# A third order for the opening of a fused linear-attention kernel: products made in terms beside the scans, and unit 0 worked under the first substitution

## The chip, the cores and the metric

The kernel runs on one core of a Trainium2 chip. The metric is the device time of one execution in microseconds (us). All data is 32-bit floating point (f32). The engines are called as the profile calls them: PE (TensorE, matrix products; PEld is its loading of weights), DVE (VectorE), ACT (ScalarE), POOL (GpSimd), and SP (SyncE), which in this kernel issues nearly all DMA transfers. Each engine works through its own queue in order; an instruction that waits holds up everything behind it on that engine.

## The reference, cut to what matters

The inputs are x and fside (4 batches of 512 tokens by 512 channels), cond (4 by 128) and weights. Two blocks follow each other, `x = x + attn(cond1(x))` and `x = x + ffn(cond2(x))`:

```python
# condition ("bi-wkv"): k = v = fside; scans over the tokens, forwards and backwards
decay = exp(-exp(w)) * (0.5 + 0.5 * tf);   ek = exp(min(k, 30));   ekv = ek * v
nf, df = scan(a = a * decay + ekv, b = b * decay + ek)     # and nb, db from the other end
euk = exp(min(u + k, 30))
out = sigmoid(x) * (nf + nb - ekv + euk * v) / max(df + db - ek + euk, 1e-8) * (0.8 + 0.2 * tf)

# attention: 16 query/key heads, 32 value heads of 128
qkvz = c @ W_qkvz.T;  beta, g = sigmoid(b), -exp(A_log) * softplus(a + dt_bias)  # from c @ W_ba.T
q, k, v = silu(causal_conv_of_4_taps(qkv));  q, k normalised
# chunks of tokens: M = strictly lower part of (k beta) k^T * decays, T = (1 + M)^-1,
# then a recurrence over the chunks with a state of 128 x 128 per value head
out = (norm(core) * norm_w * silu(z)) @ W_out.T
```

The ffn is a product with binarised weights. What the change touches is the first batch's condition, the gates (beta, g), and the first heads of the attention.

## The kernel before, in words

The work is cut into 64 *units*: four batches by 16 query/key heads, each unit with its key, query, two values and two z slices. A unit needs four *projections* of 128 weights by 512 tokens (r = 0 query, 1 key, 2 and 3 the values), each four products of 128x128 by 128x512 that add in a PSUM bank (`project`, halves 0 and 1 of two products each), and its z products (`z_product`). In the first batch the weight *slab* of 128 rows is loaded (`slab_start`, raw tile of a pool `ld` with four buffers), transposed on PE (`slab_turn`), copied by ACT (`slab_end`) and stored to a DRAM scratch `wsc` for the later batches; load and store are both issued by SP.

The convolution is `tap` 0 on ACT and taps 1 to 3 on DVE (`taps`); `silu`, `square` and the norm's sum (`norms`, `norms_copy`, `norms_turn`) follow. For a key, `key_norm` and `key_root` make an inverse square root (three Newton steps of four small POOL operations, `root`) and `key_factors` its products with the gates. `gap_load` brings the unit's cumulated decays by a broadcast DMA (512 KB), from a DRAM tile `gsc` that the gates write once per batch; `gap_mask` (POOL, 128x1024) and `gap_exp` (ACT, eight exponentials of 128x128 with a bias each) make decay matrices of them, "d" for keys (`dkd`) and "t" for queries (`dkt`). `key_pairs` (PE) and `key_matrix` (DVE, 8 steps) give M, and `key_blocks` writes its diagonal blocks of 32 to DRAM (four DMAs).

The inverse of M is made in two stages. For each *group* of four units, `group_load` brings all 128 diagonal blocks, one per partition, and `group_step` runs a substitution over 30 columns, two small operations each; `group_end` writes the result back. `inverse_load` (seven DMAs) brings the blocks of a unit, and `inverse_1` to `inverse_4`, each a set of small products on PE with a copy on DVE behind it, build the inverse of the whole chunk from them. Then the chunks follow (`chunk_r`, `chunk_w`, `chunk_t`): product with the state, product with the inverse (`ps_w`), new state and output. ACT and DVE make the steps between.

The order is written out by hand. `InOrder` keeps every engine's instructions in program order, apart from what the framework moves within its own constraints; `plan` lists in 21 lines (*slots*) what one *iteration* i does for several units at once: the chunks of unit i-1 (C), the values, query and inverse of unit i (F), the key of unit i+6 (K, `AHEAD`), the end of unit i-2 and the output product of unit i-3. `jobs` adds single items to a slot.

Before iteration 0 stands an *opening*, since nothing is there yet to overlap:

- the first batch's condition for its four columns of 128 channels (`first_turn` to `first_end`): transposes of fside and x on PE, exponentials on ACT, four scans of 128x512 per column on DVE, products on POOL, the sums of the scans as products with the identity on PE (`first_sum`: three terms each, `ps_d_first` and `ps_n_first`), a reciprocal on DVE, and the result in `cT`. The slabs of six keys are turned among it (`slab_turn(turned, 1)`);
- the gates of batch 0: `gates_product` over all four columns (`ps_ba`), `gates_exp`, `gates_series` (first beta, then a logarithm's series on DVE), `gates_sum`, `gates_keep`, `gates_turn`, `gates_rows` (the write to `gsc`);
- the keys of units 0 to 3 (*group 0*) and of 4 and 5 (*others*): `first_key`, `first_conv`, `first_silu`, `first_norm`, `first_root`; the matrices of group 0; its substitution on DVE; the norms and matrices of the others around it;
- then iteration 0, which makes the values, query and inverse of unit 0 and the key of unit 6, with the inverse moved behind slot 18 (`later`). The z products of unit 0 come in iteration 1.

In the profile L80 is the line of `InOrder`'s lambda, so that nearly every instruction has that line and is told by its tile: `lent_*` the condition's tiles, `wraw`/`wsc`/`w` a slab raw, stored and turned, `ps_p` projections, `ps_kk` key pairs, `L`, `t`, `Lt` the substitution, `ps_i` and `ps_j` the inverse's steps, `ps_w` both the turned slabs and the products with the inverse.

Of the kernel before, what the change touches and what calls it, by code (L numbers as in the profile page):

```python
# [9 lines left out]
F32 = mybir.dt.float32  # L10
# [30 lines left out]
def kernel(  # L41
# [104 lines left out]
    with ExitStack() as main:  # L146
# [24 lines left out]
        for cb in range(KT):  # L171
            at = slice(cb * P, (cb + 1) * P)
            raw = ld.tile([P, NC, P], F32, tag="raw", name=f"raw_k_first_{cb}")
            for t, src in ((raw, fside), (xs[0][:, :, at], x)):
                A.dma_start(out=t, in_=src[0, :, at].rearrange("(c p) d -> p c d", p=P))
            first_raw[cb] = raw

# [4 lines left out]
        for n, v in enumerate((w1, w2, u1, u2)):  # L182
            Q.dma_start(out=wu[:, n, :], in_=v.rearrange("(n p) -> p n", p=P))
        Q.dma_start(out=alog, in_=A_log.partition_broadcast(P))
# [17 lines left out]
        A.activation(nea, alog, AF.Exp)  # L202
        V.tensor_scalar_mul(nea, nea, -1.0)

# [127 lines left out]

        def gates_series(g):

            b, y, e = g["b"], g["y"], g["e"]
            V.tensor_scalar_add(beta[b], beta[b], 1.0)
            V.reciprocal(beta[b], beta[b])
# [21 lines left out]
        def gates_keep(g):  # L359
# [13 lines left out]
                gsum[b][:, 0].rearrange("p c (q r) -> p q c r", r=2),  # L373
            )

        def gates_turn(g):
            g["pt"] = bank("pj", f"ps_gt_{g['b']}")
            T.transpose(g["pt"][: NC * HV, :P], g["flat"][:, : NC * HV], ident)

        def gates_rows(g):  # L380
            b, n = g["b"], NC * HV
            rows = wkp.tile([P, S], F32, tag="d", name=f"sp_r_{b}")
            A.copy(rows[:n, :P], g["pt"][:n, :P])
# [137 lines left out]
        def root(v, y, t):  # L521
            for _ in range(3):
                G.tensor_tensor(t, y, y, ALU.mult)
                G.tensor_tensor(t, t, v, ALU.mult)
                G.tensor_scalar(t, t, -0.5, 1.5, ALU.mult, ALU.add)
                G.tensor_tensor(y, y, t, ALU.mult)
# [491 lines left out]
        def last_add(b, c):  # L1018
# [79 lines left out]
        INVERSE = (  # L1098
            inverse_1, inverse_1_end, inverse_2, inverse_2_end, inverse_3, inverse_3_end,
            inverse_4, inverse_4_end,  # L1100
        )

# [27 lines left out]
        for i in range(2):  # L1130
            homes.append(u2p.tile([P, S], F32, tag="q", name=f"lent_q_{i}"))

# [10 lines left out]
        def first_bound(w):  # L1143
# [3 lines left out]
            w["nf"] = w["ek"]  # L1147
# [14 lines left out]
        def first_scan(w, what):  # L1162
            dec = decay[:, 0, w["cb"], 0:1].to_broadcast([P, S])
            src = w["ek" if what == "d" else "ekv"]
            V.tensor_tensor_scan(w[what + "f"], dec, src, 0.0, ALU.mult, ALU.add)
            V.tensor_tensor_scan(
                backwards(w[what + "b"]), dec, backwards(src), 0.0, ALU.mult, ALU.add
            )

        def first_mix(w):  # L1170
            G.tensor_tensor(w["ekv"], w["ek"], w["k"], ALU.mult)
            G.tensor_tensor(w["d"], w["d"], w["ek"], ALU.subtract)
            G.tensor_tensor(w["k"], w["d"], w["k"], ALU.mult)

        def first_sum(w, what):
            ps = w["sum_" + what] = bank("st", f"ps_{what}_first_{w['cb']}")
            parts = (w["d" if what == "d" else "k"], w[what + "f"], w[what + "b"])
            for i, part in enumerate(parts):
                T.matmul(ps, lhsT=ident, rhs=part, start=(i == 0), stop=(i == 2))

        def first_end(w):
# [5 lines left out]

        work = []
        stages = (
            first_turn, first_bound, first_limit, first_x, first_mix, (first_scan, "d"), (first_sum, "d"),  # L1190
            (first_scan, "n"), (first_sum, "n"), first_end,
        )
        for cb in range(KT):
            w = wkv_start(0, 0, cb)
            for i, f in enumerate(stages):
                work.append((i + 4 * cb, cb, f, w))
        turned = 0
        for i, (_, cb, f, w) in enumerate(sorted(work, key=lambda s: s[:2])):
            f, *args = f if isinstance(f, tuple) else (f,)
            f(w, *args)  # L1200
            if i % 6 == 5 and turned < AHEAD:
                if turned == 0:
                    for n in range(AHEAD):
                        if n < 2:
                            slab_start(n, 1, homes[n])
                if turned + 2 < AHEAD:
                    slab_start(turned + 2, 1, homes[turned + 2])
                slab_turn(turned, 1)
                slab_end(turned, 1)
                turned += 1  # L1210
        for n in range(turned, AHEAD):
            slab_turn(n, 1)
            slab_end(n, 1)


        wba_raw = ld.tile([2 * HV, D], F32, tag="raw", name="wba_raw")
        Q.dma_start(out=wba_raw, in_=W_ba)
        wbaT = wp.tile([P, KT, 2 * HV], F32, name="wbaT")
        ps = bank("pj", "ps_wba")
        for k in range(KT):  # L1220
            T.transpose(
                ps[:, k * 2 * HV : (k + 1) * 2 * HV], wba_raw[:, k * P : (k + 1) * P],
                ident[: 2 * HV, : 2 * HV],
            )
        A.copy(wbaT.rearrange("p k o -> p (k o)"), ps[:, : KT * 2 * HV])

        cw = wp.tile([P, 4 * HQ, 4], F32, name="cw")
        Q.dma_start(out=cw, in_=conv_w.rearrange("(n p) k -> p n k", p=P))
        g = {"b": 0}

        def first_key(n, tag="pp"):
            project(n, 1, 0, tag)
            project(n, 1, 1, tag)

        def first_conv(n):
            tap(n, 1, 0)
            taps(n, 1)

# [213 lines left out]
```

## Time and profile before

| | us |
|---|---|
| median of 3 runs (lowest to highest) | 3196.23 (3192.85 to 3197.49) |
| the profiled execution: its time | 3197.57 |
| its span | 3195.8 |
| PE busy in the span | 3069.3 (96%), 20058 instructions |
| DVE busy | 2044.6 (64%) |
| ACT busy | 1861.6 (58%), of it 137 table loads 175.8 |
| POOL busy | 1329.4 (42%) |
| mean granted PE clock over the span | 0.981 |

The profile is one execution. Times in it count from the span's start. A product's idle time is put down to what released it; PE's matrix products of f32 show as two records each. A granted clock below 1.00 means that PE ran slower in that stretch. The page's 40 slices are 80 us each: PE's busy tenths are 6, 4, 8 in the first three and 9 in all others but the last, which has 8.

### The profile page before, as it was taken

To read this page: it belongs to the slowest core of one execution; us is meant where nothing else is said; L and a number is where in the kernel's file an instruction comes from. 1 tells how busy PE (TensorE), PEld (TensorE's weight loads), DVE (VectorE), ACT (ScalarE), POOL (GpSimd) and SP (SyncE) were. 2 spreads that over 40 slices of the span, in tenths; PEclk is the share of its full clock that TensorE was granted. 3 is DMA by queue.
4 is the path that set the end of the run, shared out by engine and by line. 5 is a ranking of instruction groups with operands and counts; after the bars stand their busy time and mean duration, and the time that the engine had idled before them with its cause. 6 is when DMAs were issued, how large, how long until landed. Compare 5 with 4: busy or idle time off the path is not lost.

```text
span 3195.8 us, 57474 instructions
## 1 busy us (share of the span) xinstructions
PE 3069.3 (96%) x20058; PEld 2055.2 (64%) x20058; DVE 2044.6 (64%) x4454; ACT 1861.6 (58%) x5115; POOL 1329.4 (42%) x3042
## 2 busy tenths in 40 slices
PE   6489999999999999999999999999999999999998
PEld 3356766666766666666666666666666666665664
DVE  7545767666655776667655686667755656577542
ACT  2446666666666666556565666556666555655542
POOL 3216354263522646264432646255442515255302
PEclk9689999999999999999999999999999999999999
DMA  3334444444434323332332323323332332333321
GB/s 74 95 87 130 141 127 119 124 125 128 132 109 142 115 59 106 86 96 78 108 102 78 116 86 83 111 77 95 112 92 76 104 86 86 105 90 93 105 83 53
DMA packets 418800, 320.49 MB, mean 100 GB/s; under 512 B 217104, under 2 KB 326160, under 8 KB 418128
## 3 DMA queue, kind: packets, MB, share of 16 engines
q1 hardware_dynamic: 414288, 314.72, 33.6%
q8 instruction: 160, 2.62, 0.3%
q10 hardware_dynamic: 4224, 2.10, 0.2%
q14 instruction: 128, 1.05, 0.1%
HBM read 246.19 MB, written 70.52 MB: 99 GB/s over the span
## 4 chain that ended last, share of the span: by engine, by line
PE 80%; DVE 11%; ACT 3%; DMA 3%; issue 1%; SPq 1%; ACTq 0%; POOL 0%; DVEq 0%; POOLq 0%
PE ps_p L80 24%; PE ps_out L80 12%; PE ps_z L80 12%; PE ps_w L80 4%; PE ps_s L80 4%; PE ps_i L80 3%; PE ps_o L80 3%; PE ps_j L80 3%; DVE y L80 3%; PE ps_st L80 2%; PE ps_kq L80 2%; PE ps_f L80 2%; DVE f L80 2%; PE ps_h L80 1%; PE ps_v L80 1%
## 5 line engine op out<-in xcount | busy, mean ns | idle before, releaser
L80 PE MATMUL ps_p<-cT,w 128*128 128x512 f32 x2000 | 956.4, 606 | 8.4 <-ACT w L80 8.4
L80 DVE SCALAR_TENSOR_TENSOR y<-ps_p,cw,y 128x511 f32<-128x511 f32 (+2 forms) x768 | 570.9, 743 | 419.3 <-ACT y L80 405.6
L80 PEld LDWEIGHTS ps_p<-cT,w 128*128 128x128 f32 x2000 | 346.9, 191 | 302.0 <-issue 270.8
L80 PE MATMUL ps_z<-w,cT 128*128 128x256 f32 x2048 | 476.5, 379 | 0.0
L80 PE MATMUL ps_out<-wo,hT 128*128 128x512 f32 x1024 | 466.8, 599 | 7.3 <-DMA wo<-wosc 7.3
L80 PEld LDWEIGHTS ps_z<-w,cT 128*128 128x128 f32 x2048 | 373.7, 190 | 42.5
L80 PEld LDWEIGHTS ps_out<-wo,hT 128*128 128x128 f32 x1024 | 186.0, 191 | 195.8 <-issue 189.0
L80 POOL TENSOR_TENSOR L<-L,t 128x30 f32<-128x30 f32 (+14 forms) x450 | 270.4, 601 | 35.3
L80 ACT ACT_TABLE_LOAD x137 | 175.8, 1283 | 154.0 <-DVE y L80 116.0
L80 ACT ACTIVATE qs<-ps_s,eg 128x128 f32<-128x128 f32 x384 | 120.5, 366 | 229.5 <-DVE r L80 121.9
L80 POOL TENSOR_TENSOR t<-L 128x30 f32<-128x30 f32 (+14 forms) x450 | 228.7, 508 | 34.5 <-DMA L<-blocks_m 3.3
L80 POOL TENSOR_TENSOR rs_t_o<-rs_y_o 128x8 f32<-128x8 f32 x192 | 38.5, 201 | 461.0 <-DVE rs_y_o L80 450.0
L80 ACT ACTIVATE y<-ps_p,cw 128x512 f32<-128x512 f32 x256 | 174.1, 680 | 90.2 <-PE ps_p L80 90.1
L80 POOL TENSOR_SCALAR_AFFINE_SELECT dkd<-dkd 128x1024 f32<-128x1024 f32 x64 | 70.5, 1101 | 350.4 <-DMA dkd<-gsc 223.0
L80 ACT ACTIVATE dkt<-dkt,gsum 128x128 f32<-128x128 f32 x512 | 162.9, 392 | 69.3 <-POOL dkt L80 68.9
L80 DVE TENSOR_TENSOR x<-x,ps_out 128x512 f32<-128x512 f32 x256 | 168.9, 679 | 32.8 <-PE ps_out L80 32.6
L80 POOL TENSOR_TENSOR rs_t_k<-rs_y_k 128x4 f32<-128x4 f32 x174 | 48.3, 277 | 328.4 <-DVE rs_y_k L80 319.3
L80 DVE SCALAR_TENSOR_TENSOR o<-o,rs_y_o,nz 128x128 f32<-128x128 f32 x512 | 183.0, 412 | 0.1
L80 DVE SCALAR_TENSOR_TENSOR r<-ps_s,nbe,vb 128x128 f32<-128x128 f32 x384 | 115.9, 343 | 96.8 <-PE ps_s L80 96.7
L80 ACT ACTIVATE junk<-o 128x128 f32<-128x128 f32 x512 | 158.0, 309 | 31.8 <-DVE o L80 23.6
L80 DVE TENSOR_TENSOR o<-ps_o,qs 128x256 f32<-128x256 f32 x192 | 80.8, 421 | 144.1 <-PE ps_o L80 136.1
L80 ACT ACTIVATE wd<-ps_w,eg 128x128 f32<-128x128 f32 x384 | 119.7, 364 | 87.8 <-PE ps_w L80 87.5
(270 smaller groups left out, 5771.3 us busy)
## 6 DMA issues: line engine op xcount, KB each, us to landing
w<-wsc SPq DMA_DIRECT2D x288, 256.0 KB, 5.3
dkd<-gsc SPq DMA_DIRECT2D x64, 512.0 KB, 4.7
dkt<-gsc SPq DMA_DIRECT2D x64, 512.0 KB, 4.5
wraw<-in_L_attn_W_qkvz_dram SPq DMA_DIRECT2D x96, 256.0 KB, 3.0
wo<-wosc SPq DMA_DIRECT2D x96, 256.0 KB, 3.8
wsc<-w SPq DMA_DIRECT2D x90, 256.0 KB, 2.1
blocks_m<-dkd SPq DMA_DIRECT2D x256, 32.0 KB, 1.7
L<-blocks_m SPq DMA_DIRECT2D x16, 512.0 KB, 5.5
```

Source lines behind the costliest of these rows:

```text
L80: return lambda *args, **kw: tc.keep_in_program_order(op(*args, **kw))
```

## The change

The change rewrites the opening and removes iteration 0; from iteration 2 on the program is as before.

- Loads: ACT issues those of the first column only; SP issues the other six after `cond`, `w1`, `w2` and `u1`.
- Condition: the two subtractions per column on POOL go; `first_sum` has four terms each, the first multiplied by a tile `minus` (minus identity) on PE. All columns' transposes and exponentials come earlier (`1.5 * cb`).
- Slabs: eleven are turned in the condition, one behind each of its steps from step 4 on: keys 0 to 3, `W_ba`, unit 0's values and query (r = 2, 3, 0), keys 4 to 6.
- Gates and keys 0 to 2 are made by terms (`first_gates`, `first_key`): columns 0 and 1 together, column 2, column 3, each when the column is done, between the sums on PE.
- Gates: beta is made later (`gates_beta`), the cumulated sums are copied straight from PSUM, the transpose shares a bank, `nea` is made later (ACT, POOL).
- Keys: unit 0's value and query projections stand between the keys of group 0; the first root runs on DVE (`root(*many, V)`); keys 4 to 6 are projected under the substitution and convolved behind it.
- Under the substitution: unit 0's values, query, z products and `kq`; the inverse of unit 0 follows it directly, with the steps of keys 4 and 5 between its stages.
- Iteration 1 gets, as `jobs`, the matrices and blocks of keys 4, 5 and 6 and the remaining steps of 5 and 6; `is_made` leaves out z of unit 0 there.

```diff
-        for cb in range(KT):
+        def first_load(cb, queue):
...
+        first_load(0, A)
...
-        for n, v in enumerate((w1, w2, u1, u2)):
+        for n, v in ((0, w1), (1, w2), (2, u1)):
             Q.dma_start(out=wu[:, n, :], in_=v.rearrange("(n p) -> p n", p=P))
+        for cb in range(1, KT):
+            first_load(cb, Q)
+        Q.dma_start(out=wu[:, 3, :], in_=u2.rearrange("(n p) -> p n", p=P))
...
-                gsum[b][:, 0].rearrange("p c (q r) -> p q c r", r=2),
+                ps[:, :n].rearrange("p (c q r) -> p q c r", q=HQ, r=2),
...
-        def root(v, y, t):
+        def root(v, y, t, E=G):
...
         def first_mix(w):
             G.tensor_tensor(w["ekv"], w["ek"], w["k"], ALU.mult)
-            G.tensor_tensor(w["d"], w["d"], w["ek"], ALU.subtract)
             G.tensor_tensor(w["k"], w["d"], w["k"], ALU.mult)
...
-            parts = (w["d" if what == "d" else "k"], w[what + "f"], w[what + "b"])
+            if what == "d":
+                parts = (w["ek"], w["d"], w["df"], w["db"])
+                w["nf"] = w["ek"]
+            else:
+                parts = (w["ekv"], w["k"], w["nf"], w["nb"])
             for i, part in enumerate(parts):
-                T.matmul(ps, lhsT=ident, rhs=part, start=(i == 0), stop=(i == 2))
+                T.matmul(ps, lhsT=ident if i else minus, rhs=part, start=(i == 0), stop=(i == 3))
...
+        def first_gates(ks):
...
+            for k in ks:
+                for c in range(NC):
+                    T.matmul(
+                        ba[:, c, :], lhsT=cT[0][:, k, c * P : (c + 1) * P], rhs=wbaT[:, k, :],
+                        start=(k == c == 0), stop=(k == KT - 1 and c == NC - 1),
+                    )
...
+        def first_key(n, ks):
...
+            for k in ks:
+                T.matmul(
+                    u["pp1"], lhsT=u["w1"][:, k, :], rhs=cT[0][:, k, :], start=(k == 0),
+                    stop=(k == KT - 1),
+                )
...
+        slabs = [(lambda n=n: slab_start(n, 1, homes[n]), lambda n=n: slab_turn(n, 1), lambda n=n: slab_end(n, 1)) for n in group0]
+        slabs.append((wba_start, wba_turn, wba_end))
+        slabs += [(lambda r=r: slab_start(0, r), lambda r=r: slab_turn(0, r), lambda r=r: slab_end(0, r)) for r in (2, 3, 0)]
+        slabs += [(lambda n=n: slab_start(n, 1, homes[n]), lambda n=n: slab_turn(n, 1), lambda n=n: slab_end(n, 1)) for n in others[:2]]
+        slabs.append((lambda: slab_start(AHEAD, 1), lambda: slab_turn(AHEAD, 1), lambda: slab_end(AHEAD, 1)))
...
+        for i, f, *args in (
+            (13.5, first_gates, (0, 1)), (13.6, first_key, 0, (0, 1)), (13.7, first_key, 1, (0, 1)),
+            (13.8, first_key, 2, (0, 1)), (17.5, first_gates, (2,)), (18.1, first_key, 0, (2,)),
+            (18.2, first_key, 1, (2,)), (18.3, first_key, 2, (2,)),
+        ):
+            work.append((i, KT, f, *args))
+        loading, turning = list(slabs), list(slabs)
+        for start, *_ in slabs[:2]:
+            start()
+            loading.pop(0)
+        for i, cb, f, *args in sorted(work, key=lambda s: s[:2]):
+            f(*args)
+            if cb < KT and i >= 4 and turning:
+                if loading:
+                    loading.pop(0)[0]()
+                _, turn_it, end_it = turning.pop(0)
+                turn_it()
+                end_it()
...
+        first_silu(0)
+        tap(2, 1, 0)
+        both(project, 0, 2)
+        first_norm(0)
+        key_pairs(0, "st")
...
+        many = root_start(kn, GROUP * NC, "first")
+        root(*many, V)
...
+        tap(0, 3, 0)
+        tap(0, 0, 0)
+        taps(0, 3)
+        taps(0, 0)
...
         for j in range(1, BS - 1):
             group_step(0, j, V)
         group_end(0, V.tensor_copy)
         inverse_load(0)
         inverse_load(1)
...
+        first_conv(4)
+        inverse_1(0)
+        inverse_1_end(0)
+        inverse_2(0)
+        first_conv(5)
+        inverse_2_end(0)
...
+        for n, slot in zip(others, (0, 6, 12)):
+            job(1, slot, key_matrix, n, 0)
+            job(1, slot + 1, key_matrix, n, 1)
+            job(1, slot + 1, key_blocks, n)
+        for half in range(2):
+            job(1, 2, gap_exp, 5, "d", half)
+            job(1, 8, gap_exp, 6, "d", half)
+        job(1, 0, tap, 6, 1, 0)
+        job(1, 1, taps, 6, 1)
+        job(1, 2, silu, 6, 1)
...
-        for i in range(NU - W - 1):
+        for i in range(1, NU - W - 1):
```

## The prediction, made before the change was run

> **What bounds the kernel now.** I read the 40 slices first: from the fourth on PE is at 9, and only the first three show gaps. So a change of the opening is worth what it does until the units run at PE's pace. Then the busy time by stage, cut where the chain of waits changes hands: last column of the condition done (62.83), decays written out (77.28), blocks of the first group arrived (122.82), substitution done (145.88), first product with an inverse of unit 0 (199.12), of unit 1 (242.18), of unit 2 (290.27). Columns: stretch, its length, busy us of PE, PEld, DVE, ACT, POOL, then granted clock, DMA share, GB/s.
>
> ```profile
> 13.00:62.83 49.83, 34.34 (x98) 15.64 (x98) 49.02 (x38) 14.07 (x26) 22.21 (x12) 0.97 0.30 69
> 62.83:77.28 14.45, 11.71 (x50) 7.22 (x51) 9.37 (x27) 2.21 (x7) 0.00 (x0) 0.95 0.00 1
> 77.28:122.82 45.54, 31.86 (x113) 20.39 (x112) 20.55 (x50) 25.67 (x56) 14.15 (x36) 0.69 0.37 123
> 122.82:145.88 23.06, 8.10 (x24) 5.18 (x24) 21.00 (x63) 9.28 (x32) 0.00 (x0) 0.57 0.01 4
> 145.88:199.12 53.24, 29.53 (x198) 18.58 (x198) 19.04 (x48) 12.10 (x25) 8.16 (x37) 0.66 0.33 91
> 199.12:242.18 43.06, 42.03 (x298) 30.28 (x298) 21.69 (x51) 27.51 (x78) 5.43 (x18) 0.93 0.35 98
> 242.18:290.27 48.09, 44.05 (x314) 31.43 (x313) 23.28 (x59) 30.34 (x83) 29.23 (x70) 0.93 0.50 151
> 290.27:338.92 48.65, 48.65 (x338) 33.72 (x337) 36.27 (x73) 34.28 (x88) 29.27 (x58) 1.00 0.48 144
> ```
>
> DVE carries the sums (49.02 of 49.83) and the substitution (21.00 of 23.06); between and after, nobody is full; from 290 on PE is. The chain (start, length, engine and tile) names the waits:
>
> ```profile
> 94.57 9.55 PE ps_p L80 x16
> ...
> 119.10 3.69 DMA L<-blocks_m
> ...
> 155.61 3.11 DMA wraw<-in_L_attn_W_qkvz_dram
> ...
> 187.71 1.08 PE ps_i L80 x32
> ```
>
> The products of keys 4 and 5 (94.57) stand before the matrices of units 0 to 3, and a slab load starts unit 0's projections only after the substitution. From the timeline:
>
> ```profile
> 18.37 5.49 PE L80 MATMUL ps_d_first<-lent_M,ident 128*128 128x512 f32 x6 [3.00 <-POOL lent_M L80]
> ...
> 24.51 2.74 PE L80 MATMUL ps_n_first<-lent_M,ident 128*128 128x512 f32 x6
> ...
> 54.51 1.40 PE L80 MATMUL ps_d_first<-lent_vb,ident 128*128 128x512 f32 x2 [3.53 <-DVE lent_vb L80]
> ...
> 62.89 3.12 PE L80 MATMUL ps_ba<-wbaT,cT 128*128 128x64 f32 x26 [0.35 <-DVE cT L80]
> ...
> 206.66 0.57 ACT L80 COPY w<-ps_w 128x512 f32<-128x512 f32 x1
> ```
>
> A 512-wide f32 product is two records: 0.86 us at full clock (six records 2.74), 1.7 at half (5.49). After 3.53 us without work the granted clock fell to 0.50; after 2.66 us (before 42.43) it did not.
>
> **The change part by part**, against the profiled execution (3197.57 us, span 3195.8; 1.3 above the median).
>
> *Sums (+9.3).* ACT now issues two loads, not eight; its first load of tables, at 10.51 before, comes at about 2, and the first exponentials at 8 to 9 (limited by the landing of u1, 2.3 plus 5.2 to 6.9) instead of 12.37. DVE begins near 9.2, not 13.0: -3.8. The six moved loads are issued by SP instead (0.4 to 0.5 each, waiting on earlier landings as ACT's did), so its first slab load goes at 10.8 instead of 10.14. The two POOL subtractions per column become `minus` products on PE; POOL still runs two products of 2.1 us beside each second pair of scans, so those stay at 2.2 us against 1.2 alone, and I credit nothing. Against it: PE's order puts four key slabs and W_ba ahead of the first sum, where one slab stood. On SP, wraw_3 stands behind the store of slab 0, and that behind ACT's copy, which now follows the exponentials of three columns (15 activations, 2.8 us per column: about 17.5). wraw_3 issues at 18, lands 2.9 later; W_ba issues behind slab 1's store at 18.8 and lands 3.1 later, 22. The first sum, four products, starts at 22.7 and ends at 26.2 (full clock) to 29.5 (half); I take 28, since PE was at half until 24.3 before. DVE, through with its scans at 17.5, waits; its first end step comes at 28 instead of 24.27: +3.7. The order of SP is thus what the early start is lost to. Next, the key terms (0,1) stand between cT(1) and the third column's sums: gates 1.9 (16 records at 0.12) + six products 5.2 + sum 3.4 = 10.5 us, where DVE is ready at 7.2 (41.25 to 48.5 before): +3.3, and up to +7 at half clock, since PE idles 3.5 us there; I take +4.3. Term 2 adds 2.6 ahead of the last sum: +0.6. Three slab transposes (0.43 each) between the first column's two sums put the second 0.7 behind the reciprocal. 3.7 + 4.3 + 0.6 + 0.7 = 9.3. Ends: -1 (slabs on time, full clock) and +13 (all cold).
>
> The page "TensorE: Matmul & The Clock Gate" of the Trainium skill (Part 4) says that transposes do not count as work for the clock. By it the dense slab transposes would leave PE at half and the first sum at 29.5, 1.5 us more; no row here parts the two.
>
> *Gates (-3.3).* Of the gates' 32 records the first 24 are made beside the sums, so behind the last column stand 8 at 0.12, not 26 (3.12): -2.2. `gates_beta` behind the series: -0.6 (68.01 less 67.4). `sp_f` from PSUM without waiting for the copy: -0.5. Keys 0 to 3 (2.6 + 3.4) lie beside the series' 7 us on PE. Ends -2 and -4.
>
> *Keys to blocks (-5.3).* From the decays' write: DVE's taps for 1, 2, 3 and for unit 0's value hide nothing late. PE: value product from +0.6, cold after the gap (eight records 6.2), norm 0.95 and pairs 0.93, product 3.4, norm, pairs, product 3.4, norms: the norms are ready at +20.4. Root on DVE: three ops and twelve at 0.2, 3.1; POOL factors 0.9; 32 matrix steps 8.9 (as at 107.10); blocks out and in 6.8 (115.99 to 122.82): +40.2 against 45.5. ACT's 32 exponentials end at +22.6, POOL's seven masks (1.09 each, loads 1.3 apart) at +16.5 (two slab loads, put between the decay loads on SP, are in that): both beside it. The two unit-0 products before the norms are what is late now; without them -12. With PE at half throughout: +4.
>
> *Substitution (0).* The same 60 steps, 23.1. Under it go unit 0's z (four products 6.9), transposes and keys 4 to 6 (10.3): about 25 us of PE, from +27 to +56 after the write, done before +63.
>
> *To the first inverse product (-34.3).* From Lt: blocks 2.9, seven loads at 0.49 (2.95), landing 2.2: 8.2. The inverse chain took 9.5 (187.71 to 197.2); taps of key 5 stand before its second copy on DVE: +1.2. 18.9 against 53.24. Ends -31 (waiting on the loads for unit 1 too) and -37.
>
> *Unit 0's chunks, iteration 1 (+12).* PE loses z (6.9) and two slabs (0.9), gains two pairs (1.8) and norms: 37 us if PE were full. It will not be. DVE: key 4's matrix is first in the queue and waits for POOL's root, which starts late and has two masks inside: to +4.6; then eight matrix steps 2.2, taps of key 6 2.3, small ops 0.8: the state copy comes at +10.3, not +3.0 (202.15). ACT: two groups of eight exponentials (2.45 each), activations of key 6 (2.0) and, of the iteration's six table loads (two before, at 201.12 and 215.02), three before slab 7's copy, which comes at +16.3, not +7.5 (206.66), and PE waits behind it, cold when it resumes; key 6's exponentials and two loads push key 7's square and the next slab, so that unit 1's second projection starts at +36.7, not +21.0. From there 22 us less z and slabs, latency-bound, 19: 56. I take 55. Ends 40 (ACT's own work, 39) and 58.
>
> A table load is 1.28 us in this trace, the next activation starting at once (104.85 and 106.14): four make 5.1. "ScalarE: Activation LUTs" of the Trainium skill (What ACT_TABLE_LOAD costs) counts 2.66 per switch with its drain; by that the sum would be 5.5 worse. The row decides.
>
> *Iteration 2 (+3).* Blocks of key 7, then seven inverse loads, then unit 2's decays on SP come about 3.5 later against PE. It waits there already (250.79, 3.39 idle). Ends 0 and +6. Later iterations have the same instructions.
>
> Sum: 9.3 - 3.3 - 5.3 + 0 - 34.3 + 12 + 3 = -18.6. 3197.6 - 18.6 = 3179.0; taken from the median, 3177.6. I say 3178.
>
> **Rivals.**
> 1. *The fill works:* slabs arrive in time, PE stays warm, iteration 1 runs near ACT's own 40 us. Sums +2, gates -3.3, keys -8, inverse -35, iteration 1 -1, iteration 2 +2: -43, 3154. For it: 29.5 of the 53 us before the first inverse product were PE's, and that work is now under the substitution. Against: the orders above.
> 2. *It gives the gain back:* sums at +13, keys -1, iteration 1 +15, iteration 2 +6, with -3.3 and -34.3: -4.6, 3192. For it: every queue has more in front of it in just these stages.
> 3. *Slower, by slabs one at a time:* eleven slabs must pass PE before the second column's sum. If SP's store-before-load order leaves one in flight, a trip is 0.43 + 2.9 + 1.1 + 0.6 + 0.33 = 5.4 us, 59 in all, and that sum comes at 70 instead of 41: +29, total +10, 3207. It decides from trips of 5.0 us on (25 us late). Against: the order lets two be in flight, and loads were 2.9 us.
> 4. *No effect,* for PE is at 96% of the span: 3196. Against it: PE had no work for 23.7 of the 53.24 us from 145.88.
>
> **How the numbers follow.** Forecast (-33 to -6.4) 0.69; rival 1 0.15; rivals 2 and 4 0.09; rival 3 0.07. A measurement of this kernel tells about 0.2%, 6.4 us, from none. Faster 0.84, same 0.09, slower 0.07. The range cuts a tenth below and a tenth above: 3160 to 3191.
>
> **What would show it.** The last column's end near 71; `ps_d_first` first at 22 to 23, behind `ps_wba`; gsc near 82; L near 122; first `ps_i` near 154 and inverse product near 164; a PE gap of several us before `ps_p` of key 7 with ACT as releaser; unit 1's inverse product near 219. I am wrong if slabs come earlier (sums then end at 62) or if iteration 1 keeps PE full.

## The result, and the profile after

The changed kernel takes 3182.40 us (median of 7 runs, 3176.15 to 3188.74) against 3196.23 (median of 7, 3192.85 to 3201.87): a ratio of 0.9956, 95% interval 0.9944 to 0.9969. It is faster by 0.44%, and the interval lies below 1. The forecast was 3178, range 3160 to 3191.

The profiled execution took 3176.15 us (span 3174.2). It is the fastest of the seven; what that means is settled by one of the runs below. First the busy time by stage of this execution, cut at the same events as before: last column of the condition done (75.13), decays written (86.57), blocks of the first group arrived (124.63), substitution done (147.75), first product with an inverse of unit 0 (167.83), of unit 1 (222.51), of unit 2 (272.12). Columns as before: stretch, length, busy us of PE, PEld, DVE, ACT, POOL, granted clock, DMA share, GB/s.

```profile
13.00:75.13 62.13, 50.81 (x158) 27.49 (x158) 39.75 (x32) 11.61 (x22) 9.44 (x7) 0.89 0.41 91
75.13:86.57 11.44, 8.37 (x29) 4.35 (x29) 7.82 (x24) 2.77 (x8) 0.30 (x1) 1.00 0.00 1
86.57:124.63 38.06, 30.63 (x116) 17.78 (x116) 25.67 (x68) 25.39 (x61) 11.90 (x24) 0.87 0.49 161
124.63:147.75 23.12, 14.62 (x64) 10.56 (x64) 21.04 (x63) 9.97 (x24) 0.00 (x0) 0.86 0.09 28
147.75:167.83 20.08, 9.76 (x138) 8.05 (x138) 8.91 (x17) 4.80 (x8) 3.29 (x13) 0.50 0.48 137
167.83:222.51 54.68, 42.33 (x283) 27.83 (x283) 27.78 (x78) 37.85 (x99) 12.82 (x55) 0.81 0.19 54
222.51:272.12 49.61, 44.91 (x314) 32.16 (x314) 24.81 (x62) 29.85 (x82) 29.22 (x70) 0.92 0.51 152
```

In the first stretch the roles have changed: DVE had 49.02 of 49.83 us and now has 39.75 of 62.13, and PE has 50.81, so the three columns that became longer now wait for PE. The substitution has 14.62 us of PE under it, not 8.10. The stretch from 145.88 to 199.12, 53.24 us long, has become one of 20.08. The next one has grown from 43.06 to 54.68, with ACT at 37.85. Against the prediction (us; stage lengths after less before):

| stage | predicted | measured |
|---|---|---|
| sums | +9.3 | +12.3 |
| gates | -3.3 | -3.0 |
| keys to blocks | -5.3 | -7.5 |
| substitution | 0 | +0.1 |
| to the first inverse product | -34.3 | -33.2 |
| iteration 1 | +12 | +11.6 |
| iteration 2 | +3 | +1.5 |
| sum | -18.6 | -18.2 |

The sums, column by column (`cT` written, from DVE's timeline): first column at 29.18 before, 33.44 after; then 12.07, 12.07 and 9.51 us for the next three before, and 12.08, 16.46 and 13.14 after. The first column waits for its sum on PE, which stands behind `W_ba`:

```profile
23.84 0.43 PE L80 MATMUL ps_wba<-ident,wba_raw 64*128 64x64 f32 x4 [1.56 <-ACT cT L80]
24.20 1.13 PE L80 MATMUL ps_d_first<-lent_M,lent_ekv 128*128 128x512 f32 x2
25.16 2.74 PE L80 MATMUL ps_d_first<-lent_M,ident 128*128 128x512 f32 x6
...
32.69 0.75 DVE L80 SCALAR_TENSOR_TENSOR cT<-ps_n_first,scale,lent_M 128x512 f32<-128x512 f32 x1 [0.67 <-PE ps_n_first L80]
```

From 145 on the chain of waits (start, length, engine and tile) runs through the loads of the inverse, PE at half clock, and then ACT:

```profile
147.75 2.87 DMA blocks_t<-Lt
...
153.46 1.86 DMA inv_t<-blocks_t
155.37 1.07 PE ps_i L80 x30
...
165.96 2.08 PE ps_kk L80 x8
168.03 0.87 PE ps_w L80 x4
...
171.72 3.15 ACT dkd L80 x11
...
176.52 1.28 ACT L80
...
179.12 1.28 ACT L80
180.42 1.28 ACT dkt L80 x4
```

ACT makes 16 exponentials, key 6's activations between two loads of tables (1.28 each), and only then the copy of slab 7; PE waits 3.13 us and resumes cold, that is at half clock, four records in 3.40 us where 1.9 is the full pace:

```profile
182.33 0.57 ACT L80 COPY w<-ps_w 128x512 f32<-128x512 f32 x1
...
182.94 3.40 PE L80 MATMUL ps_p<-cT,w 128*128 128x512 f32 x4 [3.13 <-ACT w L80]
```

### The profile page after: what moved, and what is told of

The parts are those of the page before. It is cut to its first block, busy times and chain, and to the rows that moved or that the text cites. A ratio compares the mean times of both kernels' runs of the same rounds, so it can differ in the third digit from the quotient of the medians.

```text
span 3174.2 us, 57532 instructions
## 1 busy us (share of the span) xinstructions
PE 3071.4 (97%) x20076; PEld 2054.9 (65%) x20076; DVE 2046.0 (64%) x4468; ACT 1867.0 (59%) x5121; POOL 1319.8 (42%) x3040
## 4 chain that ended last, share of the span: by engine, by line
PE 80%; DVE 10%; ACT 3%; DMA 3%; issue 1%; SPq 1%; POOL 0%; ACTq 0%; DVEq 0%; POOLq 0%
PE ps_p L80 24%; PE ps_out L80 12%; PE ps_z L80 12%; PE ps_w L80 4%; PE ps_s L80 4%; PE ps_i L80 3%; PE ps_o L80 3%; PE ps_j L80 3%; DVE y L80 3%; PE ps_st L80 2%; PE ps_kq L80 2%; DVE f L80 2%; PE ps_f L80 2%; PE ps_h L80 1%; PE ps_kk L80 1%; PE ps_v L80 1%
## 5 line engine op out<-in xcount | busy, mean ns | idle before, releaser
L80 DVE TENSOR_TENSOR x<-x,ps_out 128x512 f32<-128x512 f32 x256 | 168.9, 679 | 34.3 <-PE ps_out L80 33.9
```

Source lines behind the costliest of these rows:

```text
L80: return lambda *args, **kw: tc.keep_in_program_order(op(*args, **kw))
```

## The experiments

All are edits of the changed kernel and compute all of it. Times are medians, with the ratio to the kernel before beside it and its 95% interval; the kernel before took 3195.17 beside e1, e2, e4 and e5, 3198.39 beside e7, e3, e9 and e10, and 3198.13 beside e11 to e14.

**e1, the first sum ahead of the slabs.**

```diff
-            if cb < KT and i >= 4 and turning:
+            if cb < KT and i >= 6 and turning:
```

> The slabs are turned behind the steps from the first column's first sum on, not from two steps earlier, so that this sum stands on PE ahead of four key slabs and W_ba. My theory (the early start of the condition is lost because the first sum waits behind slab loads in SP's order): the first sum starts near 13 to 15 instead of 24.2, the first column ends near 23 instead of 33.4, and the last near 65 to 67 instead of 75.1; the whole gains 8 to 10 us on the changed kernel, since nothing behind the condition changes. Rival (the eleven slabs have to pass somewhere, and the wait only moves from the first column to the second): the second column ends near 43 to 45 as now, the last at 73 to 75, and the whole gains 0 to 2 us.

Measured: 3184.06 us (ratio to before 0.9962, 0.9947 to 0.9977), nothing gained. The first column ended at 23.84, 9.6 us earlier, and the second at 47.39, 1.9 later than in the changed kernel (and later than the 43 to 45 of the rival), the last at 75.52. So the rival's outcome held; its cause is another, as SP's queue and e7 show. PE and SP in the second column of e1:

```profile
26.80 1.08 PE L80 MATMUL ps_w<-ident,wraw 128*128 128x128 f32 x4 [0.76 <-DMA wraw<-in_L_attn_W_qkvz_dram]
32.92 1.08 PE L80 MATMUL ps_w<-ident,wraw 128*128 128x128 f32 x4 [5.04 <-DMA wraw<-in_L_attn_W_qkvz_dram]
33.80 1.92 PE L80 MATMUL ps_d_first<-lent_M,lent_ekv 128*128 128x512 f32 x2
```
```profile
24.73 0.43 SPq L80 DMA_DIRECT2D cw<-in_L_attn_conv_w_dram  x1
25.25 5.08 SPq L80 DMA_DIRECT2D wraw<-in_L_attn_W_qkvz_dram  x1
31.89 0.38 SPq L80 DMA_DIRECT2D cw<-in_L_attn_conv_w_dram  x1
32.36 4.76 SPq L80 DMA_DIRECT2D wraw<-in_L_attn_W_qkvz_dram  x1
```

PE waits 5.04 us for a slab whose load took SP 5.08 us to issue, where others take 0.4; from the end of that issue to PE's start are 2.6 us, no more than the 3.0 in which a slab's load usually lands. In front of it stands `cw`, the weights of the convolution, and it stands there twice: the change issues it at `if i == 8`, and two work items have that number (the first column's second sum, and the second column's `first_mix`, 4 + 4). A gap on PE ended by DMA is thus read one queue further back: the slab itself was not slow, its issue was.

**e7, as e1 with `cw` once, behind the slabs.**

```diff
-            if i == 8:
-                Q.dma_start(out=cw, in_=conv_w.rearrange("(n p) k -> p n k", p=P))
+        Q.dma_start(out=cw, in_=conv_w.rearrange("(n p) k -> p n k", p=P))
         assert not turning
```

> As e1, and the load of the convolution's weights (cw), which the change issues twice in the middle of the slabs and which held the next transfer on SP for 4.8 to 5.1 us each time in e1, is issued once, behind all slab loads. My theory now (e1 gained nothing because the slabs of the second column came late, and they came late because of these two loads): the first column ends near 24 as in e1, the second at 37 to 41 instead of 47.4, the last at 65 to 69, and the whole is 6 to 9 us faster than the changed kernel, about 3173 to 3176. Rival (a slab's trip itself is too long, whatever stands in SP): the second column ends at 45 or later and the whole stays within 2 us of the changed kernel.

Measured: 3174.00 us (0.9929, 0.9914 to 0.9944), 8.4 less than the changed kernel. The columns ended at 24.22, 41.13, 56.29 and 67.74: the first, second and last are where I had expected them, the second at the upper edge. At unit 2's inverse product its profile is 4.9 us ahead of the changed kernel's first one, and 7.0 ahead of that of e12. The same slab now waits 1.1 us, not 5:

```profile
28.74 1.09 PE L80 MATMUL ps_w<-ident,wraw 128*128 128x128 f32 x4 [1.12 <-DMA wraw<-in_L_attn_W_qkvz_dram]
29.62 1.91 PE L80 MATMUL ps_d_first<-lent_M,lent_ekv 128*128 128x512 f32 x2
31.33 4.26 PE L80 MATMUL ps_d_first<-lent_M,ident 128*128 128x512 f32 x6
```

**e11, `cw` once, the first sum where the change has it** (the second edit of e7 alone).

> The changed kernel with the weights of the convolution loaded once, behind all slabs, and the first sum left where the change has it. In the trace of the changed kernel the two loads held only stores up (SP 35.1 to 40.0 and 42.1 to 46.8), all slab loads were out by 31.8. My theory (the double load costs only together with an early first sum): columns, decays and total as in the changed kernel, within 2 us. Rival (it takes part in the changed kernel's time too, by the DMA engines or by the fourth column's work): 3 us faster or more.

Measured: 3182.51 us (0.9950, 0.9935 to 0.9966); the columns ended at 34.47, 46.55, 63.04 and 74.48. No effect alone, as expected: the two edits pay only together. Here, where two waits lie one behind the other, an experiment on either alone shows nothing.

**e2, the keys' products behind the last column.**

```diff
-            (13.5, first_gates, (0, 1)), (13.6, first_key, 0, (0, 1)), (13.7, first_key, 1, (0, 1)),
-            (13.8, first_key, 2, (0, 1)), (17.5, first_gates, (2,)), (18.1, first_key, 0, (2,)),
-            (18.2, first_key, 1, (2,)), (18.3, first_key, 2, (2,)),
+            (13.5, first_gates, (0, 1)), (17.5, first_gates, (2,)),
...
-            first_key(n, (3,) if n < 3 else (0, 1, 2, 3))
+            first_key(n, (0, 1, 2, 3))
```

> The products of keys 0 to 2 are not made by terms between the sums but all four terms behind the last column; the gates stay as the change has them. My theory: the terms cost the sums about what they save later. The third column's sum starts near 47 instead of 53.4, the last column ends 7 to 8 us earlier (67 to 68), but the gates' sums then wait behind 16 key products (13.8 us at full clock) and the decays are written at 83 to 86 instead of 86.6: the whole moves by -4 to +1 us. Rival (the terms fill holes of PE and are what the new opening gains from): the decays are written at 90 or later and the whole is 4 to 8 us slower than the changed kernel.

Measured: 3181.03 us (0.9954, 0.9937 to 0.9971), no difference. The third column took 12.08 us, as before the change, not 16.46: the terms cost it 4.4. (In e3 and e4, with the same instructions up to there, that column took 14.77: eight records of the keys' products ran in 3.65 us, against 4.75 in the changed kernel, and those of the gates in 1.10, against 1.72. So 1.7 of the 4.4 is the clock.) Then the gates took 17.60 us and not 11.44, with PE busy for 15.86 of them, and the decays were written at 88.63, between my 83 to 86 and the rival's 90:

```profile
71.03:88.63 17.60, 15.86 (x47) 7.86 (x47) 7.82 (x25) 2.99 (x8) 0.30 (x1) 1.00 0.00 0
```

The products by terms, the change's most visible part, move PE's work from behind the last column to before it and are worth nothing that can be measured by themselves.

**e13, the subtractions on POOL again.**

```diff
             G.tensor_tensor(w["ekv"], w["ek"], w["k"], ALU.mult)
+            G.tensor_tensor(w["d"], w["d"], w["ek"], ALU.subtract)
             G.tensor_tensor(w["k"], w["d"], w["k"], ALU.mult)
...
-                parts = (w["ek"], w["d"], w["df"], w["db"])
+                parts = (w["d"], w["df"], w["db"])
...
-                parts = (w["ekv"], w["k"], w["nf"], w["nb"])
+                parts = (w["k"], w["nf"], w["nb"])
...
-                T.matmul(ps, lhsT=ident if i else minus, rhs=part, start=(i == 0), stop=(i == 3))
+                T.matmul(ps, lhsT=ident, rhs=part, start=(i == 0), stop=(i == 2))
```

> One part of the change undone: the subtraction of ek from the second exponential is made on POOL again, once per column, and both sums have three terms on PE, none with minus identity. If moving it to PE is worth something (POOL's products slow DVE's scans from 1.2 to 2.2 us), the columns come 1 to 3 us later each and the whole is 3 to 8 us slower. If PE is the busier of the two between the columns, as I read the changed kernel's third and fourth column, the two products (0.86 us each, half of their cost when cold) leave the path and the last column ends 0 to 4 us earlier; the whole -4 to +1 us. I take the second.

Measured: 3179.09 us (0.9949, 0.9933 to 0.9965): 2 to 3 us less than the changed kernel, which the times alone can't tell from nothing. The columns can: 33.21, then 12.08, 16.80 and 9.72 us. The fourth is back to nearly the 9.51 of before, where the changed kernel took 13.14. In the changed kernel it begins with the product by `minus`, at half clock:

```profile
62.03 1.16 PE L80 MATMUL ps_ba<-wbaT,cT 128*128 128x64 f32 x8 [1.61 <-DVE cT L80]
62.98 2.02 PE L80 MATMUL ps_d_first<-lent_vb,lent_ekv 128*128 128x512 f32 x2
64.80 2.66 PE L80 MATMUL ps_d_first<-lent_vb,ident 128*128 128x512 f32 x4
```

So taking work from POOL to PE cost time in the fourth column. It gained none in the others. In the second, where DVE sets the pace, both kernels take 12.08 us. In the third DVE waits for PE in e13 too, and the column is no shorter without the products by `minus`, since eight key records before the sum ran longer at half clock (5.72 us, against 4.75 in the changed kernel):

```profile
57.15 0.69 DVE L80 SCALAR_TENSOR_TENSOR lent_o<-ps_d_first,cT 128x512 f32<-128x512 f32 x1 [4.62 <-PE ps_d_first L80]
```

**e5, the substitution ahead of unit 0's taps.**

```diff
         group_load(0)
+        for j in range(1, BS - 1):
+            group_step(0, j, V)
+        group_end(0, V.tensor_copy)
+        inverse_load(0)
         tap(0, 3, 0)
         tap(0, 0, 0)
         taps(0, 3)
...
-        for j in range(1, BS - 1):
-            group_step(0, j, V)
-        group_end(0, V.tensor_copy)
-        inverse_load(0)
         inverse_load(1)
```

> On DVE the substitution stands before the taps of unit 0's second value and query, so that what hangs on them (activations, slab copies of z, z products, transposes, norms, key 6's projection) can only run behind the substitution; nothing else moves. My theory (most of what the change gains is that this work lies under the substitution): the first inverse product of unit 0 starts at 182 to 188 instead of 167.8, and the whole is 13 to 18 us slower than the changed kernel, about the kernel before. Rival (the gain comes from having the inverse follow at once, and the work finds room in the starved iteration 1): the whole is less than 6 us slower.

Measured: 3203.09 us, slower than the kernel before (1.0027, 1.0017 to 1.0038). PE makes nothing in the 23.12 us of the substitution (it made 14.62 in the changed kernel), and the stage behind it takes 40.83 us instead of 20.08:

```profile
128.58:151.70 23.12, 0.00 (x0) 0.00 (x0) 21.03 (x63) 0.00 (x0) 0.00 (x0) 0.53 0.01 5
151.70:192.53 40.83, 24.71 (x202) 18.81 (x202) 13.40 (x23) 16.09 (x32) 4.05 (x16) 0.67 0.28 80
```

Unit 0's inverse product came at 192.53, behind my 182 to 188, 3.95 of it because the substitution itself ended later here (151.70, not 147.75). The work under the substitution is worth 20.7 us, more than all that the change gains, and more than my 13 to 18. The clock is not the reason: PE is busy for 24.71 us in this stage, and for 14.62 and 9.76 us, 24.38 together, in the two stages of the changed kernel. It is the order:

```profile
158.51 6.39 PE L80 MATMUL ps_z<-w,cT 128*128 128x256 f32 x16 [31.49 <-ACT w L80]
...
174.04 0.69 PE L80 MATMUL ps_i<-inv_t,dkd 32*32 32x32 f32 x32
```

DVE's taps and ACT's steps hold PE's first product up for 6.8 us, the fill then takes PE 15.5 us, and only behind it come the inverse's steps. These take 18.5 us to the inverse product, not 12.5, since ACT and DVE have key 4's exponentials, taps and activations between them (171.55 to 180.93 on the chain of waits).

**e3, e4, e9, e14: iteration 1.** e3 moves the exponentials of keys 4 to 6:

```diff
         both(gap_exp, 0, "t")
+        for n in others:
+            both(gap_exp, n, "d")
...
-        both(gap_exp, 4, "d")
         for j in range(1, BS - 1):
...
-            job(1, 2, gap_exp, 5, "d", half)
-            job(1, 8, gap_exp, 6, "d", half)
```

> Of e4 only the exponentials: those of keys 4 to 6 stand behind those of unit 0's query, where ACT is idle; the convolutions, norms and roots stay as the change has them. My theory (ACT's queue paces iteration 1, and e4's gain comes from taking work out of it, each part with its time): 2.45 us less stand before the copy of slab 7, 2.45 and two loads of tables less before the copy after it, so the stretch between the inverse products of units 0 and 1 is 51 to 53 us, against 54.7 in the changed kernel and 49.1 in e4. Rival (the roots and norms, on POOL and DVE, were what held e4's part back): 54 to 55 us, nothing gained.

e4 has that too, and the convolutions, norms and roots of keys 4 to 6 around the stages of unit 0's inverse, with the jobs of iteration 1 that made them gone:

```diff
-        first_conv(4)
+        for n in (4, 5):
+            tap(n, 1, 0)
+            taps(n, 1)
+        silu(4, 1)
+        first_square(4, homes[2])
+        tap(6, 1, 0)
+        taps(6, 1)
...
         inverse_2_end(0)
+        key_norm(4)
+        key_root(4)
...
         inverse_4_end(0)
+        key_norm(6)
+        key_root(6)
...
-        job(1, 0, tap, 6, 1, 0)
-        job(1, 1, taps, 6, 1)
-        job(1, 2, silu, 6, 1)
```

> The exponentials of keys 4 to 6 stand behind those of unit 0's query (ACT idle there from 114.6 to 122.2), and the convolutions, norms and roots of keys 4, 5 and 6 all stand before and between the stages of unit 0's inverse instead of partly in iteration 1. My theory (iteration 1 is long because ACT reaches the copy of slab 7 late, behind 16 exponentials, key 6's activations and three loads of tables): that copy comes at 175 to 177 instead of 182.3, PE's idle time before key 7's projection shrinks from 3.1 to about nothing, unit 1's inverse product starts at 210 to 214 instead of 222.5, and the whole gains 8 to 11 us on the changed kernel. Rival (iteration 1 is paced by the slab's trip from DRAM through PE, ACT and back, or by DVE): unit 1's inverse product at 219 or later, a gain under 3 us.

e9 is e4 with slab 7 turned and copied before the inverse, and no longer in iteration 1:

```diff
         first_square(6, homes[5])
+        slab_turn(AHEAD + 1, 1)
+        slab_end(AHEAD + 1, 1)
         inverse_1(0)
```

> As e4, and slab 7 (loaded since 96) is turned on PE and copied by ACT before unit 0's inverse instead of behind the exponentials of iteration 1. My theory (in e4 the copy came at 179.6, held up by ACT waiting 2.4 us for a mask on POOL behind three roots, so PE still waited 2.9 us for it and ran at half clock behind it): key 7's first product follows the first state products at once, near 177 instead of 180.2, at full clock (2.0 for its two products, not 3.8), and the stretch between the inverse products of units 0 and 1 is 42 to 45 us instead of 49.1; the whole gains 4 to 7 us on e4. Rival (the chunks of unit 0, a chain over PE, ACT and DVE, pace the iteration): 47 to 49 us, nothing gained.

Measured, with the stage from unit 0's inverse product to unit 1's, and when in it key 7's first product starts:

| | time, us | stage, us | key 7's product at | clock |
|---|---|---|---|---|
| changed kernel | 3182.40 | 54.68 | +15.1 | 0.81 |
| e3 | 3178.32 (0.9946, 0.9930 to 0.9963) | 53.04 | +13.5 | 0.85 |
| e4 | 3172.81 (0.9932, 0.9916 to 0.9947) | 49.09 | +10.5 | 0.85 |
| e9 | 3171.45 (0.9920, 0.9905 to 0.9935) | 46.00 | +7.8 | 0.83 |

The stage gets shorter with each step, by 8.7 us in all, so ACT's queue did pace it. The times of the kernels follow less exactly: e9's is only 1.4 below e4's, where I had expected 4 to 7. In e4 unit 1's inverse product came at 218.79, nearer the rival's 219 than my 210 to 214. Of the 9.6 us by which e4's time fell, 5.6 lie in this stage, where I had expected 8.5 to 12.5; behind unit 2's product its profile takes 2899.2 us, the other profiles 2902 to 2909, so the rest can be spread between executions. The stage gained less than expected since ACT waited for POOL's mask, which three roots now preceded, and came to the copy only at 179.6:

```profile
175.36 2.44 ACT L80 ACTIVATE dkd<-dkd,gsum 128x128 f32<-128x128 f32 x8 [2.38 <-POOL dkd L80]
179.61 0.56 ACT L80 COPY w<-ps_w 128x512 f32<-128x512 f32 x1
```

e9 takes the copy out of the way and key 7's product starts when I said (176.84), but still at half clock (3.78 for four records), and the stage is 1 us longer than my bounds.

**e10, e7 and e9 together.**

> e7 and e9 together. If the opening's sums and iteration 1 are separate stages in series, their gains add: 13 to 17 us less than the changed kernel's 3182, so 3165 to 3169. If something common (the first slabs, PE's clock, the steady pace behind) decides, the two overlap: 3170 to 3176.

Measured: 3164.99 us (0.9899, 0.9885 to 0.9914), the best version but for e14, which equals it: 33 us below the kernel before beside it and 17 below the changed one. The sums end at 66.13 and the stage of iteration 1 takes 46.08 us, so the two gains, 8.4 and 11.0, add up to within 2 us.

**e14, e10 with key 6's norm and root in iteration 1.**

```diff
-        key_norm(6)
-        key_root(6)
         gap_load(AHEAD + 1, "d")
...
+        for f in (key_norm, key_root):
+            job(1, 6, f, 6)
```

> As e10, but key 6's norm and root (4.3 us of POOL) go back from the opening to the middle of iteration 1, since ACT waited 4.6 us there for POOL's mask of key 7, behind that root. If this wait still paces the iteration: the stretch between the inverse products of units 0 and 1 is 43 to 44.5 us instead of 46.1, the whole 1 to 3 us less than e10's 3165. If PE's own work paces it by now: 46 us, no change.

Measured: 3164.86 us (0.9897, 0.9877 to 0.9916), no difference, though the stage fell to 41.41 us, further than I had expected:

```profile
161.23:202.64 41.41, 35.69 (x269) 24.33 (x269) 25.57 (x72) 25.44 (x74) 11.13 (x43) 0.95 0.26 65
```

The granted clock is 0.95 where e10 has 0.83; but in this execution the sums ended 2.6 us later than in e10's (a fourth column of 13.15 us, not 11.45). At unit 2's product it is 3.5 us ahead of e10 (252.63 against 256.16), but its span is 0.6 us longer. Whether the order or the clock's luck made the shorter stage stays open.

**e12, the changed kernel again, unedited.**

> The changed kernel once more, unedited. Its seven times go from 3176.2 to 3188.7 and its profile is of the fastest. In the runs that share its opening up to the first sum (e2, e3, e4, e5, e9) the first column ended at 35.1 to 37.0, not at 33.4. If the spread comes from the start of the opening: another median of 3179 to 3185, and a profile with the first column at 35 to 37 and a span of 3177 to 3183. If not, the first column ends near 33.4 whatever the span is.

Measured: 3181.21 us (0.9950, 0.9930 to 0.9970), and a profile of 3183.6 us, 9.4 longer than the first. The first column ended at 34.46, below my 35 to 37, and my guess on the spread was mostly wrong. At unit 2's inverse product this execution is only 2.2 us behind (274.29 against 272.12), and from there to the end it loses 7.2 more, in a few single iterations. The largest such steps, 3.1 and 3.2 us, are in units 13 and 60. Unit 13's stretch in the first profile, and in this one:

```profile
761.38:810.10 48.72, 47.97 (x330) 32.97 (x329) 34.36 (x72) 31.43 (x85) 17.60 (x37) 1.00 0.38 116
```
```profile
763.14:814.95 51.81, 49.71 (x330) 33.56 (x329) 34.38 (x72) 31.42 (x85) 17.64 (x38) 0.97 0.39 110
```

and what PE waited for in it, the first profile and then this one (us in total, times, longest):

```profile
PE ps_i L80 <- DMA inv_t<-blocks_t: 0.8, 1, 0.8
```
```profile
PE ps_i L80 <- DMA inv_t<-blocks_t: 2.1, 1, 2.1
```

A wait of 0.8 us left the clock at 1.00; one of 2.1 us was followed by a stretch at a lower clock and cost 3.1. So the first profile's span is a lucky one, and the medians are the measure: 3182.40, 3181.21 and (e11, equal in effect) 3182.51.

## Why the prediction was right, and where it was not

The forecast went the right way, by the mechanism it named, and its sum was within 0.5 us of the first profile at unit 2's product. Three profiles of the changed kernel (the first, e12 and e11, equal in effect) are 18.2, 16.0 and 15.9 us ahead of the kernel before there, so the sum of -18.6 was 0.5 to 2.7 us too good. Behind it they take 2902.1, 2909.3 and 2905.4 us, and the kernel before took 2905.5: what is left of the 4.4 us between 3178 and 3182.4 can't be told from this spread. Some of the agreement is luck, since errors of both signs cancel: the sums came 3.0 us worse than forecast and the inverse 1.1, the keys 2.2 better and iteration 2 1.5. The times that the prediction lists as signs (71, 82, 122, 164, 219) lie 1 to 2 us below what its own sum gives; the terms are compared here.

- **First column.** `ps_d_first` was to start at 22.7 behind `W_ba` and end at 28; it started at 24.20 and ended at 27.9. That the early start is lost to the slabs was right, and e1 and e7 show its worth: 9.6 us in that column, and at the last one, once `cw` is out of the way, 7.4 against the first profile and 6.7 against e12.
- **Third column.** +4.3 was predicted for the key terms and +4.4 came, and e2 gives them back exactly. 1.7 of it is the clock, which e3 and e4 did not lose.
- **Fourth column.** +0.6 was predicted and +3.6 came. This is the step that failed. The forecast counts the products by `minus` in the first sum ("four products") and in the third ("sum 3.4"), and says "I credit nothing" for POOL's relief; but the fourth column's term has only the 2.6 us of the key terms in it, and nothing for these products, where PE ended last. By e13 the fourth column without them takes 9.72 us, with the key terms in place; with them 11.45 in e12 (+1.73, two products of 0.86) and 13.14 in the profile (a further 1.7 at half clock).
- **Gates.** They took 11.44 us; 11.15 was forecast.
- **Keys.** -5.3 was predicted and -7.5 came: the norms were ready at +18.9 from the decays' write (20.4 in the forecast), since the first value product took 5.10 us and not 6.2; the first matrix began at +23.0 (24.4), and the blocks were there at +38.1 (40.2). Each step was put a little high; none was missing.
- **To the first inverse product.** The stage took 20.08 us, not 18.9. From the end of the substitution the last of the loads came at +7.6 (8.2), and the inverse's steps took 10.6 (10.7), at a clock of 0.50 from end to end as before the change. What I had overlooked is key 4's pairs, which stand right before the product (2.08 us). That the fill is the gain is shown by e5.
- **Iteration 1.** It took 54.68 us, and 55 was forecast. The copy of slab 7 came at +14.5, not +16.3, PE resumed cold, and unit 1's second projection started at +34.5 (36.7). e3, e4 and e9 confirm ACT's queue, and show what I had not written: behind it POOL's masks were next in line.
- **Rivals.** The first (the fill works, slabs in time, ACT's own pace, 3154) is what e10 goes towards, at 3165. The second had the sums right (+13) but the keys gained 7.5 and not 1, and iterations 1 and 2 lost 13.1 and not 21. The third, the slabs holding the second column up, did not happen in the changed kernel, but e1 has it. It came by SP's queue and not by trips of 5 us: e1's second column took 23.55 us instead of 12.08, and 16.91 in e7, so `cw` made 6.6 of the 11.5. The other 4.8 I have not taken apart.

## What to carry to other kernels

Work moved under a serial stretch of another engine can be worth more than its own busy time there (20.7 us against 14.62 here), for behind that stretch its waits lie on the path too. A piece moved from one engine to another costs time in a stage that ends on a wait for the receiver. When moving an operation earlier gains nothing, look at the next wait in line and at what stands in the queue that issues the transfer it waits for; two such blocks may have to be removed together before either shows, as here. Take a difference of some microseconds from stage lengths in several profiles, not from one span.

## What the runs showed of the hardware

- A load of 128 KB in 16-byte pieces (`cw`) took 7.0 us to land and held up the next issue in SP's queue for 4.8 to 5.1 us, where an issue usually takes 0.4 (e1; the line is that on `cw`'s issues):

```profile
DMA to landing us min/median/max: 6.9/7.0/7.1
```

  "DMA: Bandwidth & Descriptors" of the Trainium skill (Why small descriptors are slow) states a fixed cost per packet and 32 bytes of metadata per operation; that the issuing queue stands still as well is shown here only by the trace.
- The same fourth column, with the same instructions, took 11.4 us in six of the profiles and 13.1 in five, by the clock that PE had after a wait of 1.6 us. In the five, PE ran part of that column at half clock. In e12 the product by `minus`, 2.02 us long in the first profile, ran at full clock:

```profile
63.99 1.08 PE L80 MATMUL ps_d_first<-lent_vb,lent_ekv 128*128 128x512 f32 x2
```

  "TensorE: Matmul & The Clock Gate" of the Trainium skill (Part 1) says that the window that decides is free-running, so that the transition depends on where in it the work lands; that fits, but no run here shows the window itself.
- A load of tables took 1.28 us again, the next activation starting at once (176.52 and 177.81). "ScalarE: Activation LUTs" of the Trainium skill (What ACT_TABLE_LOAD costs) gives the same for the load, and a drain on top of it, 2.66 us together; the drain does not show in these traces.
- The prediction set a rule of the clock-gate page ("TensorE: Matmul & The Clock Gate", Part 4) against the trace, that transposes don't count as work for the clock. Between 16.34 and 24 us the changed kernel's PE had nothing but transposes of f32, and the granted clock went from 0.50 to 1.00 among them. In e1, with transposes alone since 6.11, four of the same shape took 1.09 us at 11.31 and 0.63 at 13.02. For these transposes the measurement speaks against the rule:

```profile
18.00:20.00 2.00, 2.00 (x11) 2.00 (x10) 0.00 (x0) 0.08 (x1) 0.00 (x0) 0.50 0.60 156
...
22.00:24.00 2.00, 0.44 (x5) 0.21 (x5) 0.00 (x0) 1.97 (x5) 0.00 (x0) 1.00 0.52 186
```
